# Attention scores as F32 products on 32 rows per head, in place of split products on 128 rows

## The chip, the cores and the metric

The kernel runs on one core of a Trainium2 chip. Its time is the device time of one execution in microseconds (us), less is better. TensorE (PE) multiplies matrices into PSUM, VectorE (DVE), ScalarE (ACT) and GpSimd (POOL) work on tiles, SyncE (SP) issues most DMAs.

## The reference

One transformer block with modulation by a condition, on x of 2 x 2048 x 512, with 16 heads of 32 columns:

```python
mod = jax.nn.silu(condition) @ Wada + bada
sh_a, sc_a, gt_a, sh_m, sc_m, gt_m = jnp.split(mod, 6, axis=1)
xn = _layernorm(x, g1, be1)
xm = xn * (1.0 + sc_a[:, None, :]) + sh_a[:, None, :]
x = x + gt_a[:, None, :] * _attention(xm, Wqkv, Wproj, bproj)
xn = _layernorm(x, g2, be2)
xm = xn * (1.0 + sc_m[:, None, :]) + sh_m[:, None, :]
h = jax.nn.gelu(xm @ W1 + b1, approximate=False)
x = x + gt_m[:, None, :] * (h @ W2 + b2)
```

`_attention` is causal softmax attention: scores of a head are the product of Q (scaled by 32 ** -0.5) and K over 32 columns, masked, exponentiated after the row's maximum is taken off, normalised, and multiplied with V. All inputs are F32.

## The kernel before, in words

The two batches are worked one after the other: a stage that makes Q, K and V (`Qkv.run`, in groups of 512 tokens), an attention stage (`attention_phase`), and a projection (`project_phase`), which for the first batch overlaps the start of the second batch's Q, K, V stage. A feed-forward stage for all tokens comes last. TensorE's products are kept in the order in which the program issues them (`mm`), so the order is written out by hand.

**Q and K.** Each tile of 128 features by 512 tokens is split by `keep` (L854) into a high part and a low part, both F32R: ScalarE copies the high part (L858), VectorE makes the rest (L859), a DMA stores both to `qd` or `kd` in DRAM (L864). `load_keys` and `load_queries` read them back with one head's 32 columns repeated as four row groups, so that the 128 rows of a product hold the four combinations of high and low: the F32R product of `kst` and `qst` on 128 rows is one head's score.

**Attention.** A unit is one of four groups of four heads (`c`) and one block of 512 queries (`i`): 16 units a batch, 32 in all. Each unit has a step per tile of 128 keys, 4i + 3 in all, because the last four tiles are masked and share three steps. In a step (`scores_t`, L574):

- `fold` and `sel`: four BF16 products on 32 rows each, one per head, write minus the row's maximum into the four `st` banks. The maximum stands as three BF16 parts (`split`, L487) in `mhl`, transposed into `fold` by `rows` (L539).
- four `st` products (one per head) add the transposed scores; ScalarE's exponential (L620) turns each into `e`; GpSimd masks the diagonal (L629).
- Between them `row.score` (L517) issues some `s` products: scores not transposed, of units up to three ahead, from which VectorE takes the maximum of each row (L484, masked L479). `count` and `due` set how many fall into a step. They have two PSUM banks of their own, and now and then one of `st`.
- `values` (`o`) multiplies V with `e` of two steps before, and `row_sums` (`sm`) sums `e`: four F32 products each, the four heads in column groups of 32. The order in which these wait is the list `pending`, emptied by `flush` at the end of each step. For unmasked tiles GpSimd first adds the `e` of four key tiles (`begin_chain`, `add_to`, L650), so that one `sm` product serves four.

Scores of the first units are made in the Q, K, V stage already (`among` in `run`): after a projection's product one `s` or two are issued. `sevens` (L964) makes two by two blocks of Q and K by seven products instead of eight and hands its sums to `keep`.

Of the kernel before, what the change touches and what calls it, by code (L numbers as in the profile page):

```python
# [27 lines left out]
def dit_block_kernel(  # L28
# [49 lines left out]
    EE_BUFS = 8  # L78
# [25 lines left out]
    sel = bp.tile([P, P], BF16, tag="sel", name="sel")  # L104
    ident_h = bp.tile([P, P], BF16, tag="ident_h", name="ident_h")
    nc.vector.tensor_copy(ident_h, ident)
# [9 lines left out]
    fold, mhl = [], []  # L116
    for n in range(2):

        f = bp.tile([P, QB + P], BF16, tag=f"fold{n}", name=f"fold{n}")
        fold.append(f)  # L120
    for n in range(AHEAD + 1):
        m = bp.tile([P, HC, HD], BF16, tag=f"mhl{n}", name=f"mhl{n}")
        nc.vector.memset(m, 0.0)
        mhl.append(m)
# [5 lines left out]
    def picks():  # L130
# [32 lines left out]
    qd = [  # L163
        [dram.tile([2, P, T], F32, tag=f"q{b}{c}", name=f"q{b}{c}") for c in range(C)]
        for b in range(B)
    ]
    kd = [
        [dram.tile([2, P, T], F32, tag=f"k{b}{c}", name=f"k{b}{c}") for c in range(C)]
        for b in range(B)
    ]  # L170
# [141 lines left out]
    class Row:  # L312


        def __init__(self, b):
            self.b = b
            self.vv = bp.tile([P, NT, D], F32, tag="vv", name="vv")
            self.kst, self.qst, self.pools = {}, {}, {0: bp}
            self.at = 0
            self.todo = [  # L320
                (u, h, t, kb)
                for u, (_, i) in enumerate(units)
                for h in range(HC)
                for t in range(TQ)
                for kb in range(i + 1)
            ]
            self.mx = None
            self.spent = 0
            self.rows_made = 0

        def load_keys(self, c, g, n=1):

            tok = slice(g * MT, (g + n) * MT)
            if g == 0:
                self.kst[c] = self.pools[c % 2].tile(
                    [P, HC, T], F32R, tag=f"kst{c % 2}", name="kst"
                )
            for r in range(4):
                nc.sync.dma_start(
                    self.kst[c][r * HD : (r + 1) * HD, :, tok].bitcast(F32),  # L340
                    kd[self.b][c][r % 2, :, tok].rearrange("(h d) t -> d h t", d=HD),
                )

        def load_queries(self, u):
            c, i = units[u]
            t = bp.tile([P, HC, QB], F32R, tag="qst", name="qst", bufs=AHEAD + 1)
            for r in range(4):
                nc.sync.dma_start(
                    t[r * HD : (r + 1) * HD].bitcast(F32),
                    qd[self.b][c][r // 2, :, i * QB : (i + 1) * QB].rearrange(  # L350
                        "(h d) t -> d h t", d=HD
                    ),
                )
            self.qst[u] = t
# [48 lines left out]
        def old_queries(self):  # L403

            t = bp.tile([P, HC, QB], F32R, tag="qst", name="qst", bufs=AHEAD + 1)
            return t.bitcast(F32)

        def prefetch(self):

            st = bp.tile([P, HC, T], F32R, tag="kst0", name="kst")
            st = st.bitcast(F32).rearrange("p h t -> p (h t)")
            self.at_s = [
                st[:, n * C * QB : (n + 1) * C * QB].rearrange("p (c q) -> p c q", c=C)
                for n in range(2)
            ]  # L420
            self.xt_s = [st[:, (2 * C + n) * QB : (2 * C + n + 1) * QB] for n in range(TQ)]
            self.wproj = st[:, 3 * C * QB :].rearrange("p (c d) -> p c d", c=C)
            t = self.old_queries()
# [14 lines left out]
        def prepare(self, n):  # L438
# [3 lines left out]
            elif n == 5:  # L442
                ps = rows_of(ps_sp, 0, self.b, "s")
                self.rb_s = [self.old_queries() for _ in range(2)]
# [20 lines left out]
        def bank(self, u, h, t, kb, s):  # L465
            c, i = units[u]
            w, last = self.width(u, h, t, kb)
            mx = self.mx
# [18 lines left out]
        def split(self, u, mx, s):  # L487

            hl = mhl[u % (AHEAD + 1)][:, :, : 4 * TQ].rearrange(
                "p h (t l) -> p h t l", l=4
            )
            mx = mx.rearrange("p (h t) n -> p h t n", h=HC)
            m, rest = [
                s[:, n * HC * TQ : (n + 1) * HC * TQ].rearrange("p (h t) -> p h t", h=HC)
                for n in range(2)
            ]  # L500
            nc.vector.tensor_reduce(m, mx, axis=AX.X, op=ALU.max)
            nc.vector.tensor_reduce(hl[:, :, :, 0], mx, axis=AX.X, op=ALU.max)
            nc.vector.tensor_tensor(rest, m, hl[:, :, :, 0], ALU.subtract)
            nc.vector.tensor_tensor(hl[:, :, :, 1], m, hl[:, :, :, 0], ALU.subtract)
            nc.vector.tensor_tensor(hl[:, :, :, 2], rest, hl[:, :, :, 1], ALU.subtract)  # L505
# [11 lines left out]
        def score(self, n, borrow=None):  # L517

            for k in range(n):
                if borrow and k % 2 == 0:
                    s = borrow()
                else:
                    s = ps_sp.tile([P, QB], F32, tag="s", name="s")
                item = self.todo.pop(0)
                u = item[0]
                if self.mx is None:
                    self.mx = bp.tile(  # L530
                        [P, HC * TQ, units[u][1] + 1], F32, tag="mx", name="mx", bufs=3
                    )
                self.bank(*item, s)
                if not self.todo or self.todo[0][0] != u:
                    self.split(u, self.mx, s)
                    self.mx = None
                    self.at += 1

        def rows(self, u):  # L539
# [3 lines left out]
            ps = ps_sp.tile([P, P], BF16, tag="s", name="ps_m")  # L543
            tc.keep_in_program_order(
                nc.tensor.transpose(
                    ps, mhl[u % (AHEAD + 1)].rearrange("p h r -> p (h r)"), ident_h
                )
            )
# [15 lines left out]
    def attention_phase(row, beside=None):  # L564
        b, vv, kst, qst = row.b, row.vv, row.kst, row.qst
        with pool(f"att{b}") as ap, pool(
            f"ps_st{b}", bufs=HC, space=PSUM
        ) as ps_stp, pool(f"ps_o{b}", space=PSUM) as ps_op:
            row.pools[1] = ap
            among = beside(ap) if beside else None  # L570

            n_bank = [0]

            def scores_t(u, step, n):  # L574

                def st_bank():

                    n_bank[0] += u == len(units) - 1
                    if n_bank[0] % 6 >= HC:
                        return ps_sp.tile([P, QB], F32, tag="s", name="st")
                    return ps_stp.tile([P, QB], F32, tag="st", name="st")
# [3 lines left out]
                q0 = tiles[0][1]  # L593
                w = sum(QB - q for _, q in tiles)
                sts, es = [], []
                for h in range(HC):
                    g = slice(h * HD, (h + 1) * HD)
                    st = st_bank()
                    mm(
                        st[:, :w], sel[g, :], fold[u % 2][g, q0 : q0 + w],  # L600
                        start=True, stop=False,
                    )
                    sts.append(st)
                after = (0, 2) if n > HC else (0, 1)
                if n > HC:
                    row.score(1)
                for h in range(HC):
                    at = 0
# [11 lines left out]
                    act(nc.scalar.activation(e[:, h % 2, :w], sts[h][:, :w], AF.Exp))  # L620
# [14 lines left out]
                    if h in after and n >= 3 or h >= HC - n and n < 3:  # L635
                        row.score(1)
                if n >= 3:
                    row.score(1, st_bank)
                    row.score(min(n, HC) - 3)
                return es, max(0, n - HC - 1)  # L640
# [42 lines left out]
            def flush(upto):  # L683
                while pending and pending[0][0] <= upto:
                    pending.pop(0)[1]()
# [25 lines left out]
            for u, (c, i) in enumerate(units):  # L711
                if NQ <= u + AHEAD < len(units):
                    row.load_queries(u + AHEAD)
                if u % NQ == 0 and c + 1 < C:
                    row.load_keys(c + 1, 0, NG)
                steps = len(steps_of[u])
                for n_step, tiles in enumerate(steps_of[u]):
# [14 lines left out]
                    es, rest = scores_t(u, n_step, n)  # L732
                    rest = len(row.todo) - rest
                    make_rows = False
                    if u + 1 < len(units) and row.rows_made == u + 1:
                        if last:
                            row.score(row.count(cum[-1], u + 1))
# [62 lines left out]
    class Qkv:  # L800
# [46 lines left out]
        def group(self, g, hp, between, among):  # L847
# [35 lines left out]
            if g == 0:  # L883
                n = 0
                for f in range(C):
# [12 lines left out]
                    if f == 0:  # L898
                        asked()
# [1272 lines left out]
```

## Time and profile before

| | |
|---|---|
| median of 3 runs | 2289.31 us (2284.49 to 2290.16) |
| profiled execution | 2284.75 us, span 2283.0 us |
| granted TensorE clock | 0.999 |
| busy: PE, DVE, ACT, POOL | 98%, 68%, 43%, 58% of the span |
| DMA | 355.66 MB, 156 GB/s over the span |

A row of a group names line, engine, operation, written and read tiles, shapes and count, then busy time in us, mean ns of one, and the idle time before it with what ended it. A row of the timeline has start, length, engine, line, operation, tiles, shape and count. `32*128` behind a product's tiles is the part of the array that it uses, rows by columns; x counts records, and an F32 product on TensorE leaves two of them, an F32R or BF16 product one. Lengths of products include their way through the array and overlap, so the time that a product holds the array is read from the start of the next.

### The profile page before, as it was taken

How to read it: one execution, taken by the hardware profiler on the slowest of the kernel's cores; microseconds unless marked ns; L12 is line 12 of the kernel's file. 1: busy time of each engine (PE TensorE's matmuls, PEld its weight loads, DVE VectorE, ACT ScalarE, POOL GpSimd, SP SyncE). 2: the span in 40 equal slices, each digit the busy share in tenths (PEclk: the TensorE clock that was granted, in tenths of full speed). 3: DMA queues.
4: the chain of work that ended last, by engine and by line, in shares of the span. 5: the costliest groups of instructions: out<-in, count | busy, mean ns of one | idle time of the engine just before them, and what ended most of it. 6: DMA issues, size and time to landing. Idle time of an engine off the chain costs nothing. (4 is left out here: it accounts for less than half of the span.)

```text
span 2283.0 us, 34365 instructions
## 1 busy us (share of the span) xinstructions
PE 2237.6 (98%) x12429; PEld 1438.2 (63%) x12429; DVE 1559.3 (68%) x3132; ACT 980.4 (43%) x1908; POOL 1316.9 (58%) x1052
## 2 busy tenths in 40 slices
PE   8999999999999999999999999999999999999998
PEld 3676555455544457654555555447888888888887
DVE  3467776776766525677777777545896876876787
ACT  3334555555555134355555555623422342252230
POOL 4363997888794552268787887463764602602510
PEclk9999999999999999999999999999999999999999
DMA  9769226262234778850512304265466554654643
GB/s 281 240 217 245 54 53 144 54 146 73 76 140 159 243 248 295 267 123 24 121 48 61 84 24 145 97 221 192 146 246 226 196 185 143 210 187 151 205 149 113
DMA packets 134146, 355.66 MB, mean 156 GB/s; under 512 B 14496, under 2 KB 33484, under 8 KB 119256
## 3 DMA queue, kind: packets, MB, share of 16 engines
q1 hardware_dynamic: 126112, 305.18, 44.9%
q0 software_dynamic: 7488, 47.74, 5.7%
q8 instruction: 98, 1.61, 0.3%
q14 instruction: 72, 0.59, 0.1%
q10 hardware_dynamic: 376, 0.55, 0.1%
HBM read 253.80 MB, written 107.48 MB: 158 GB/s over the span
## 5 line engine op out<-in xcount | busy, mean ns | idle before, releaser
L620 ACT ACTIVATE e<-st 128x512 f32<-128x512 f32 (+1 forms) x1152 | 572.9, 579 | 404.7 <-PE st L204 346.0
L484 DVE TENSOR_REDUCE mx<-s 128x1 f32<-128x512 f32 x606 | 409.4, 687 | 192.2 <-PE s L204 190.3
L650 POOL TENSOR_TENSOR ee<-ee,e 128x1024 f32<-128x1024 f32 x212 | 498.7, 2384 | 8.0 <-ACT e L620 8.0
L204 PE MATMUL s<-kst,qst 128*128 128x512 f32 (+3 forms) x1028 | 438.2, 430 | 15.3 <-DVE mx L484 8.7
L204 PE MATMUL st<-qst,kst 128*128 128x512 f32 (+3 forms) x1280 | 400.4, 377 | 0.0
L204 PE MATMUL ps_a<-sum,room 128*128 128x256 f32 x1504 | 356.8, 381 | 4.7 <-DVE c L1655 1.5
L204 PEld LDWEIGHTS ps_a<-sum,room 128*128 128x128 f32 x1504 | 281.2, 190 | 54.4 <-issue 6.0
L204 PE MATMUL o<-e,vv 128*32 128x512 f32 (+3 forms) x2560 | 303.0, 538 | 1.7 <-POOL e L629 1.5
L479 DVE CUSTOM_DVE_ANT_0 junk<-s,causal 128x512 bf16<-128x512 f32 (+3 forms) x422 | 206.9, 490 | 114.5 <-PE s L204 106.5
L204 PEld LDWEIGHTS s<-kst,qst 128*128 128x128 f32 x1028 | 193.0, 188 | 137.4 <-issue 43.6
L204 PEld LDWEIGHTS st<-qst,kst 128*128 128x128 f32 x1280 | 229.1, 188 | 63.2 <-issue 33.9
L650 POOL TENSOR_TENSOR ee<-e 128x1024 f32<-128x1024 f32 x84 | 198.2, 2380 | 112.1 <-ACT e L620 104.2
L629 POOL TENSOR_SCALAR_AFFINE_SELECT e<-e 128x256 f32<-128x256 f32 x256 | 103.9, 435 | 126.2 <-ACT e L620 124.7
L1883 POOL TENSOR_TENSOR c<-c,h 128x512 f32<-128x512 f32 x40 | 58.6, 1484 | 159.4 <-ACT c L1881 159.4
L204 PEld LDWEIGHTS <-sel 32*128 32x128 bf16 x1152 | 29.2, 90 | 190.0 <-issue 187.1
L204 PE MATMUL ps_b<-sum,room 128*128 128x256 f32 x608 | 143.6, 379 | 0.0
L204 PEld LDWEIGHTS o<-e,vv 128*32 128x32 f32 x2560 | 62.4, 108 | 100.9 <-issue 80.5
L204 PEld LDWEIGHTS ps_b<-sum,room 128*128 128x128 f32 x608 | 115.0, 190 | 15.4
L204 PE MATMUL ps_v<-wqkv,xmT 128*128 128x512 f32 x256 | 123.3, 594 | 0.0
L204 PE MATMUL st<-fold,sel 32*128 32x512 bf16 (+1 forms) x1152 | 115.3, 372 | 2.6 <-DVE mhl L505 1.3
L484 DVE TENSOR_REDUCE mx<-st 128x1 f32<-128x512 f32 x162 | 111.1, 686 | 2.8 <-PE st L204 0.4
L1528 POOL TENSOR_TENSOR sum<-xm 128x256 f32<-128x256 f32 x16 | 15.6, 974 | 152.8 <-PE ps_a L204 152.8
(231 smaller groups left out, 3276.2 us busy)
## 6 DMA issues: line engine op xcount, KB each, us to landing
qst<-q SPq DMA_DIRECT2D x128, 256.0 KB
room<-w1e SPq DMA_DIRECT2D x28, 1024.0 KB
kst<-k SPq DMA_DIRECT2D x24, 1024.0 KB
room<-w1e SPq DMA_DIRECT2D x28, 768.0 KB
room<-w2e SPq DMA_DIRECT2D x21, 1024.0 KB
q<-hl SPq DMA_DIRECT2D x32, 512.0 KB
k<-hl SPq DMA_DIRECT2D x32, 512.0 KB
room<-w2e SPq DMA_DIRECT2D x21, 768.0 KB
```

Source lines behind the costliest of these rows:

```text
L204: return tc.keep_in_program_order(nc.tensor.matmul(*args, **kw))
L479: nc.vector.tensor_tensor_reduce(junk[:, :w], s[:, :w], causal[:, QB - w :], 1.0, MASKED, ALU.add, ALU.max, m,)
L484: nc.vector.tensor_reduce(m, s[:, :w], axis=AX.X, op=ALU.max)
L620: act(nc.scalar.activation(e[:, h % 2, :w], sts[h][:, :w], AF.Exp))
L629: nc.gpsimd.affine_select(d, d, pattern=[[0, 2], [1, P]], compare_op=ALU.is_ge, fill=0.0, base=0, channel_multiplier=-1,)
L650: act(engine.tensor_tensor(dst, x, y, ALU.add))
L1528: act(engine.tensor_tensor(dst, x, y, ALU.subtract))
L1883: nc.gpsimd.tensor_tensor(c, c, piece_of(base, i, t, pair), ALU.add)
```

## The change

Q and K stay on chip as they are: `keys_and_queries` allocates four tiles `kT` and four `qT` of 128 features by 2048 tokens in F32 (features of four heads on the partitions), and the Q, K, V stage writes into them (`evict`, and `dst` in `sevens`). `keep`, `load_keys`, `load_queries`, `qd` and `kd` are gone. Every score product is an F32 product of 32 rows by 128 columns in the row group of its head. `fold`, `sel` and the row maximum become F32, with one row per head and query tile in place of three (`join` for `split`).

In a step the heads are staggered: `st` of head h, `fold` with `sel` of head h + 1 (`begin`; after the last head, the first of the next step), then `s` of head h + 2 or h + 3 if one is due (`free`). `o` of two steps before is issued after the second head (`halfway`), `sm` still at the end of the step. GpSimd's sums take two key tiles (`k = n_step % 2`), and there are 16 in place of 8 half buffers of them. `todo` holds the `s` products with the heads innermost, in the order 2, 3, 0, 1.

```diff
-    EE_BUFS = 8
+    EE_BUFS = 16
...
-    sel = bp.tile([P, P], BF16, tag="sel", name="sel")
+    sel = bp.tile([P, P], F32, tag="sel", name="sel")
...
+        def keys_and_queries(self):
+            self.kT, self.qT = [
+                [bp.tile([P, T], F32, tag=f"{n}{c}", name=f"{n}T") for c in range(C)]
+                for n in "kq"
+            ]
...
+            g = slice(h * HD, (h + 1) * HD)
             mm(
                 s[:, :w],
-                self.qst[u][:, h, t * P : (t + 1) * P],
-                self.kst[c][:, h, kb * QB : kb * QB + w],
+                self.qT[c][g, i * QB + t * P : i * QB + (t + 1) * P],
+                self.kT[c][g, kb * QB : kb * QB + w],
                 start=True,
                 stop=True,
             )
...
+            def begin(u, step, h):
+                tiles = steps_of[u][step]
+                q0, w = tiles[0][1], sum(QB - q for _, q in tiles)
+                g = slice(h * HD, (h + 1) * HD)
+                st = ps_stp.tile([P, QB], F32, tag="st", name="st")
+                mm(
+                    st[:, :w], sel[g, :], fold[u % 2][g, q0 : q0 + w],
+                    start=True, stop=False,
+                )
+                folded[u, step, h] = st
...
+                if (u, step, 0) not in folded:
+                    begin(u, step, 0)
                 for h in range(HC):
                     g = slice(h * HD, (h + 1) * HD)
-                    st = st_bank()
-                    mm(
-                        st[:, :w], sel[g, :], fold[u % 2][g, q0 : q0 + w],
-                        start=True, stop=False,
-                    )
-                    sts.append(st)
...
+                    st, at = folded.pop((u, step, h)), 0
                     for j, q in tiles:
                         mm(
-                            sts[h][:, at : at + QB - q],
-                            kst[c][:, h, j * P : (j + 1) * P],
-                            qst[u][:, h, q:],
+                            st[:, at : at + QB - q],
+                            row.kT[c][g, j * P : (j + 1) * P],
+                            row.qT[c][g, i * QB + q : (i + 1) * QB],
                             start=False, stop=at + QB - q == w,
                         )
                         at += QB - q
+                    if h + 1 < HC:
+                        begin(u, step, h + 1)
+                    elif after:
+                        begin(*after, 0)
...
+                    for left in range(n * (h + 1) // HC - n * h // HC, 0, -1):
+                        free = [(h + 2) % HC, (h + 3) % HC]
+                        row.score(n - n * (h + 1) // HC + left, free)
+                    if h == 1:
+                        halfway()
...
-                        k = n_step % TQ
+                        k = n_step % 2
                         if k == 0:
                             even = es
-                        elif k == 1:
+                        else:
                             chain = begin_chain(u, even, es)
-                        else:
-                            add_to(u, chain, es)
-                        if k == TQ - 1 and n_step + 1 < i * TQ:
+                        if k and n_step + 1 < i * TQ:
                             sums_of, wait = (chain, False), 2
...
-            def keep(ps, which, f):
...
+            def evict(ps, which, f):
+                if which:
+                    nc.vector.tensor_copy(row.kT[f][:, tok], ps)
+                else:
+                    nc.scalar.activation(row.qT[f][:, tok], ps, AF.Copy, scale=HD**-0.5)
```

More of the change, by code (lines that the diff above doesn't have):

```diff
@@ L401, in inverses @@
                 self.widen(u - 1)
-        def old_queries(self):
-            t = bp.tile([P, HC, QB], F32R, tag="qst", name="qst", bufs=AHEAD + 1)
-            return t.bitcast(F32)
         def prefetch(self):
[L415 to L423, printed above, removed]
+            self.at_s = [self.old("k0"), self.old("k1")]
+            t = self.old("k2")
+            self.xt_s = [t[:, n, :] for n in range(TQ)]
+            self.wproj = self.old("q0")
+            t = self.old("q1")
             self.next_s = [t[:, n, :] for n in range(TQ)]
@@ L568, in attention_phase @@
         ) as ps_stp, pool(f"ps_o{b}", space=PSUM) as ps_op:
-            row.pools[1] = ap
             among = beside(ap) if beside else None
[L572 to L589, printed above, removed]
+            folded = {}
```

242 lines of the change are left out of this document (92 added, 150 removed).

## The prediction

> **What bounds the kernel now.** I read the page first, then the stages by window, then single steps on the timeline of TensorE. The page:
>
> ```profile
> span 2283.0 us, 34365 instructions
> PE 2237.6 (98%) x12429; PEld 1438.2 (63%) x12429; DVE 1559.3 (68%) x3132; ACT 980.4 (43%) x1908; POOL 1316.9 (58%) x1052
> PEclk9999999999999999999999999999999999999999
> ```
>
> TensorE is busy 98% of the span at a full granted clock; no other engine passes 68%. Five windows cut the span where the kinds of product change (columns: length, PE, PEld, DVE, ACT, POOL busy, clock, DMA share, GB/s):
>
> ```profile
> 60.50:200.80 140.30, 140.15 (x590) 100.20 (x588) 85.72 (x220) 49.89 (x109) 57.06 (x72) 1.00 0.77 238
> 200.80:727.50 526.70, 517.06 (x3627) 260.58 (x3626) 373.02 (x893) 302.93 (x607) 421.58 (x306) 1.00 0.40 102
> 727.50:970.00 242.50, 239.32 (x857) 147.09 (x857) 121.80 (x294) 74.41 (x158) 105.59 (x104) 1.00 0.79 263
> 970.00:1499.00 529.00, 520.99 (x3683) 263.29 (x3683) 373.58 (x893) 304.27 (x610) 405.64 (x282) 1.00 0.32 82
> ```
>
> Attention is the second and the fourth row: 526.7 + 529.0 = 1055.7 us for 288 steps (two batches, four head groups, 3 + 7 + 11 + 15 steps), with TensorE at 98%. The first and third row are the Q, K, V stages, where TensorE is at 99%. What the change is worth is therefore read from the order in which products leave TensorE, not from the other engines. One step of attention:
>
> ```profile
> 562.36 0.47 PE L204 MATMUL s<-kst,qst 128*128 128x512 f32 x1
> 562.75 1.07 PE L204 MATMUL o<-e,vv 128*32 128x512 f32 x8
> 563.75 0.40 PE L204 MATMUL st<-fold,sel 32*128 32x512 bf16 x4
> 564.08 0.50 PE L204 MATMUL st<-qst,kst 128*128 128x512 f32 x1
> 564.41 0.39 PE L204 MATMUL s<-kst,qst 128*128 128x512 f32 x1
> 564.64 0.39 PE L204 MATMUL st<-qst,kst 128*128 128x512 f32 x1
> 564.87 0.28 PE L204 MATMUL s<-kst,qst 128*128 128x256 f32 x1
> ...
> 566.01 1.06 PE L204 MATMUL o<-e,vv 128*32 128x512 f32 x8
> 567.01 0.40 PE L204 MATMUL st<-fold,sel 32*128 32x512 bf16 x4
> ```
>
> The reader should take starts, not durations: 564.41 to 564.64, so a split (F32R) score product of 512 columns on all 128 rows takes the array 0.23 us. Four BF16 row-max products on 32 rows each (563.75 to 564.08) take 0.33 us together: all four stream at once in about the 0.23 us of one product of 512 columns, and 0.10 is the change to whole-array products. The first whole-array product behind them holds for 0.33 instead of 0.23 us, 0.10 for its weights. The step is 3.26 us. Two rounds of four F32 products, heads in column groups, from another place:
>
> ```profile
> 210.90 1.06 PE L204 MATMUL o<-e,vv 128*32 128x512 f32 x8
> 211.78 1.04 PE L204 MATMUL sm<-e,ones 128*32 128x512 f32 x8
> 212.76 0.40 PE L204 MATMUL st<-fold,sel 32*128 32x512 bf16 x4
> ```
>
> Each F32 product has two records, so x8 is four products. The round takes 0.88 us (210.90 to 211.78), and 0.98 where the kind of tiling changes behind it: 0.10 for the change. One F32 product alone is as long as the round of four:
>
> ```profile
> 76.53 1.92 PE L204 MATMUL ps_mod<-wada,sc 128*32 128x512 f32 x16
> 78.39 0.70 PE L204 MATMUL ps_u<-vv,wqkv 128*128 128x256 f32 x2
> 900.71 1.02 PE L204 MATMUL ps_u<-xmT,wqkv 128*128 128x256 f32 x4
> 901.57 1.03 PE L204 MATMUL ps_w<-vv,qst 128*128 128x256 f32 x4
> ```
>
> Four records of 256 columns on the whole array are two F32 products and take 0.86 us (900.71 to 901.57), so 512 columns take 0.86. Hence F32 costs 0.86/0.23 = 3.7 times F32R per column, and four narrow tiles give that back only if all four run at once.
>
> **The change part by part.** *Score products.* A group of 32 rows holds one head. A slot of the changed order is: scores transposed (`st`) of head h, row max (`sel`) of head h+1, then mostly one score product `s` of head h+2 or h+3. The instruction order of the changed kernel has 1152 slots: 844 with one `s` in attention, 136 with two, 171 with none (the last slot of the first batch runs into the next stage). `st` of head h+1 writes on top of the row max of h+1 in the same row group, so it starts when that ends: one F32 product per slot is serial, whatever the others do. I take the slot at the 0.88 us of the round above: 1152 x 0.88 = 1014 us. The 128 slots that are 256 wide would save some 28 us of it, and 86 slots whose `s` falls into the row group of their own `st` or `sel` give about that back.
>
> *The other rounds.* `o` stays. In rounds of 512 columns it is 272 rounds, `sm` is 104; at 0.88 us that is 239 and 92 us. Sums of two key tiles in place of four bring 48 more `sm` rounds (384 products against 192): +42, so 134 us.
>
> ```profile
> L204 PE MATMUL sm<-ee,ones 128*32 128x512 f32 x384 | 52.3, 604 | 0.0
> L650 POOL TENSOR_TENSOR ee<-ee,e 128x1024 f32<-128x1024 f32 x212 | 498.7, 2384 | 8.0 <-ACT e L620 8.0
> L484 DVE TENSOR_REDUCE mx<-s 128x1 f32<-128x512 f32 x606 | 409.4, 687 | 192.2 <-PE s L204 190.3
> L620 ACT ACTIVATE e<-st 128x512 f32<-128x512 f32 x1024 | 531.3, 603 | 366.8 <-PE st L204 316.3 <-PE s L204 27.6 <-POOL ee L650 8.9
> ```
>
> GpSimd is rid of 84 of its adds, 84 x 2.38 = 200 us, which nothing waits for while TensorE sets the pace.
>
> *Changes of tiling.* Row tiles and column tiles alternate; whole-array products all but vanish from attention. `o` now stands in the middle of a step and `sm` at its end, so the order has 404 column phases against 284. Each costs 0.10 + 0.02 to enter and 0.10 + 0.10 (change, first weights) to leave: 404 x 0.32 = 129 us. The 30 transposes of the row max on the whole array cost two changes each, some 0.5: 15 us.
>
> *Waits.* By the same prices attention before is: row max 272 rounds x 0.23 = 63, `st` 1088 (in products of 512 columns) x 0.23 = 250, `s` 960 x 0.23 = 221, changes 288 x 0.46 = 132 (0.20 behind the row max, 0.16 from 562.36 to 562.75 beyond the 0.23, 0.10 behind `o`), `o` 239, `sm` 92, transposes 5: 1002 us. Measured are 1055.7, so 54 us of waits hide between records. A slot (0.88) is longer than a reduce (0.69) or an exponential (0.60), yet `s` has two banks, and a bank is free only 0.88 + 0.69 after its product starts; everything on TensorE stands in line behind an `s` that waits for one. Two banks give one `s` per (0.88 + 0.69) / 2 = 0.79 us, under the slot, so I keep the 54 us as they are; bounds are 0 and twice that. `o` in the middle of a step reads exponentials from two steps before: over 5 us old, and nothing waits there.
>
> Attention after: 1014 + 239 + 134 + 129 + 15 + 54 = 1585 us, +529.
>
> *Score products in the Q, K, V stages.*
>
> ```profile
> 900.29 0.58 PE L204 MATMUL s<-kst,qst 128*128 128x512 f32 x1
> 902.25 0.41 PE L204 MATMUL s<-kst,qst 128*128 128x128 f32 x1
> 902.50 1.08 PE L204 MATMUL ps_w<-vv,fold 128*128 128x256 f32 x4
> 0.00:200.80 200.80, 48.47 (x81) 15.33 (x81) 47.08 (x88) 1.00 0.81 249
> 727.50:970.00 242.50, 48.13 (x81) 15.32 (x81) 47.60 (x89) 1.00 0.79 263
> ```
>
> Now a lone F32R `s` among whole-array F32 products holds the array 0.42 us at 512 columns (900.29 to 900.71) and 0.25 at 128: 0.37 at their mean of 404. The last two rows count them (PE column, tile `s` alone): 81 in each stage. The changed order has 82 in each, in 74 runs, 66 of them lone: a lone one is a row tile in a whole-array stream, so 0.68 of streaming, and a change with first weights on both sides, 4 x 0.10: 1.08. 148 x (1.08 - 0.37) - 16 x 0.37 = +99 us.
>
> *At nothing.*
>
> ```profile
> L859 DVE SCALAR_TENSOR_TENSOR hl<-ps_w,hl 128x512 fp32r<-128x512 f32 x24 | 16.3, 681 | 1.8 <-ACT hl L858 1.8
> L858 ACT ACTIVATE hl<-ps_w 128x512 fp32r<-128x512 f32 x24 | 14.3, 594 | 65.1 <-DVE ps_w L995 59.7 <-DMA q<-hl 5.1
> ```
>
> The high and low halves (64 tiles, one ScalarE pass of 0.59 and one VectorE pass of 0.68 us each), their stores to and loads from DRAM, the three-way split of the row max: all ran beside TensorE at 98 to 99%. Without them SyncE's queue no longer stands in front of the stores of `sums` and `o`, whose readers come thirteen units later. Were TensorE not the pace, 64 x 0.68 = 44 us would be their worth, a fall and not a rise. Late next is nothing that I see: VectorE loses work.
>
> Sum: the profiled execution took 2284.75 us (span 2283.0, 1.75 around it); + 529 + 99 = 2913. The median of the runs is 2289.31, 0.2% over the profiled one; I forecast **2910 us**.
>
> [...] What the trace shows of two F32 products in different groups is the first modulation, where the third of four products has to wait for its weights' DMA (records of that tile alone, PE in the second column):
>
> ```profile
> 11.10:11.16 0.06, 0.02 (x2) 0.03 (x2) 0.00 (x0) 1.00 1.06 410
> 11.89:11.92 0.03, 0.03 (x3) 0.02 (x1) 0.00 (x0) 1.00 0.72 273
> 11.98:12.01 0.03, 0.03 (x5) 0.03 (x2) 0.00 (x0) 1.00 1.10 341
> ```
>
> Two first halves run at 11.14; a third product's first half starts at 11.90; the second halves of the first two start only at 11.99. So the array lets a later product pass the waiting second half of an earlier one. [...]
>
> **The rivals.** *Better overlap.* If queued products of other row groups run ahead and the banks allow it, a step costs each row group its own three products, 3 x 0.88 = 2.64 us, in place of four slots, 3.52: 288 x 0.88 = 253 less, **2660 us**. For it: the pass shown at 11.90. Against it: two `s` banks, and column phases that make all groups meet every half step. 0.16.
>
> *Start in order.* A product per 0.44 us (half of 0.88): row max, `st` and `s` of attention are 1088 + 1088 + 960 = 3136 products of 512 columns, 3136 x 0.44 = 1380 in place of 1014: **3276 us**. Against it: the rows at 11.90. 0.08.
>
> *No overlap of row groups in F32.* 3136 x 0.88 = 2760: **4656 us**. Against it: the BF16 row, four in 0.33. 0.04.
>
> *Faster.* No row shows F32 on 32 rows. Should a product there stream in one pass, as BF16 does, a slot is 0.22 and attention 1585 - 1152 x 0.66 = 825 (VectorE's 373 in each window would still fit), and the stages between lose 24 in place of 99: 2284.75 - 231 + 24 = **2078 us**. It decides from a slot of 0.38: the loss of 529 + 99 = 628 is then won back by 1152 slots and some 114 slots' worth of lone `s`, (1152 + 114) x 0.50. Against it: F32 on 32 columns takes two records of 0.43 as on 128. 0.05. Packing alone cannot bring it: at best four in 0.88 equal F32R's 0.23 each, and the row max goes from 0.23 to 0.88 per step.
>
> **How the numbers follow.** Forecast 0.66, within which the waits (-54 or +54) and first weights that no slot hides (1152 x 0.10 = +115, or none) give 2856 to 3079. The range takes in the better overlap and its error and leaves out 3276, 4656 and 2078: **2620 to 3100 us**. This kernel's measurement can tell some 0.3% from no change. Faster 0.05, same 0.01, slower 0.94 (0.66 + 0.16 + 0.08 + 0.04).
>
> **What would show it.** Right: the two windows of attention at about 790 us each, TensorE at 98%, starts of `st` 0.88 us apart within a half step, every `st`, `sel` and `s` with two records on 32*128, the Q, K, V stages 50 us longer each, the stages behind attention unchanged. Wrong: `st` starts 0.65 apart or less (better overlap), one record per product (faster), 0.44 between neighbouring products' starts (in order), or TensorE idle in attention, with VectorE or the banks of `s` named as releaser.

## The result, and the profile after

The changed kernel took **2962.7 us** (median of 4 runs, 2961.4 to 2963.7) against 2287.7 us (4 runs, 2284.5 to 2290.2): a ratio of 1.295, with a 95% interval of 1.293 to 1.297. The forecast was 2910 us, in a range of 2620 to 3100.

The page of the kernel after:

```profile
span 2960.2 us, 41653 instructions
PE 2932.4 (99%) x16525; PEld 1565.5 (53%) x16525; DVE 1552.6 (52%) x2935; ACT 1035.1 (35%) x1876; POOL 1120.6 (38%) x968
PEclk9999999999999999999999999999999999999999
```

TensorE was at 98% and is at 99%, at a full clock, in a span that is 677 us longer. GpSimd lost 196 us of work and no other engine passes 53%, and none of that shortened the span. The same five windows as before, moved to where the kinds of product change now (length, PE, PEld, DVE, ACT, POOL busy, clock, DMA share, GB/s):

```profile
60.50:265.00 204.50, 204.50 (x678) 103.97 (x676) 72.51 (x185) 42.65 (x98) 58.94 (x73) 1.00 0.23 69
265.00:1071.00 806.00, 804.90 (x5643) 323.56 (x5645) 386.42 (x833) 339.66 (x606) 328.91 (x271) 1.00 0.11 36
1071.00:1367.00 296.00, 296.00 (x889) 146.59 (x881) 103.93 (x254) 63.94 (x141) 99.96 (x97) 1.00 0.35 126
1367.00:2176.00 809.00, 807.90 (x5655) 324.96 (x5655) 386.44 (x833) 342.48 (x611) 309.12 (x241) 1.00 0.07 23
2176.00:2960.20 784.20, 769.41 (x3525) 642.48 (x3523) 586.50 (x783) 228.74 (x388) 296.40 (x241) 1.00 0.55 184
```

Attention takes 806 + 809 = 1615 us (1055.7 before): +559. The Q, K, V stages take 204.5 and 296.0 us (140.3 and 242.5): +118. What follows attention takes 784.2 us, and took 784.0 (2283.0 - 1499.0). 559 + 118 is the whole difference of the spans, 677 us.

One half step and the column phase behind it, on the timeline of TensorE (start, length; each F32 product has two records):

```profile
622.17 0.69 PE L194 MATMUL st<-qT,kT 32*128 32x512 f32 x1
622.18 0.69 PE L194 MATMUL st<-fold,sel 32*128 32x512 f32 x1
622.19 0.71 PE L194 MATMUL s<-kT,qT 32*128 32x512 f32 x2
622.71 0.59 PE L194 MATMUL st<-qT,kT 32*128 32x512 f32 x1
622.71 0.59 PE L194 MATMUL st<-fold,sel 32*128 32x512 f32 x1
622.72 0.61 PE L194 MATMUL s<-kT,qT 32*128 32x512 f32 x2
623.14 0.59 PE L194 MATMUL st<-qT,kT 32*128 32x512 f32 x1
623.15 0.59 PE L194 MATMUL st<-fold,sel 32*128 32x512 f32 x1
623.57 0.59 PE L194 MATMUL st<-qT,kT 32*128 32x512 f32 x1
623.58 0.59 PE L194 MATMUL st<-fold,sel 32*128 32x512 f32 x1
624.10 1.07 PE L194 MATMUL sm<-ee,ones 128*32 128x512 f32 x8
625.09 0.69 PE L194 MATMUL st<-qT,kT 32*128 32x512 f32 x1
```

Read the starts. The program's order here is `st` of head 2, row max of head 3, `s` of head 0 (the first slot), then `st` of head 3, row max of head 0, `s` of head 1 (the second slot), then `sm`. At 622.17 four products start together, each in a row group of its own: `st` of head 2, the row max of head 3, and both `s`. Their second records start at 622.71 and end the slot at 623.14: 0.97 us, two records of 0.43 and some 0.1 that I put down to the first weights. The `st` of head 3, which adds to the row max in its own row group, starts only then (623.14); its slot takes 0.96 us to the column phase at 624.10, two records of 0.43 and 0.1 that I put down to the change. The `s` of head 1 stands behind that `st` in the order of instructions, and ran 0.95 us ahead of it, so in the second slot two of the four row groups are empty. Half step and column phase take 2.92 us (622.17 to 625.09).

### The profile page after: what moved, and what is told of

The parts are those of the page before. It is cut to its first block, busy times and chain, and to the rows that moved or that the text cites. A ratio compares the mean times of both kernels' runs of the same rounds, so it can differ in the third digit from the quotient of the medians.

```text
span 2960.2 us, 41653 instructions
## 1 busy us (share of the span) xinstructions
PE 2932.4 (99%) x16525; PEld 1565.5 (53%) x16525; DVE 1552.6 (52%) x2935; ACT 1035.1 (35%) x1876; POOL 1120.6 (38%) x968
## 4 chain that ended last, share of the span: by engine, by line
PE 95%; DVE 4%; issue 1%; DMA 0%; POOL 0%; ACT 0%; SPq 0%; DVEq 0%; POOLq 0%; ACTq 0%
PE st L194 25%; PE s L194 18%; PE ps_a L194 11%; PE o L194 9%; PE ps_b L194 6%; PE sm L194 5%; PE ps_v L194 4%; PE ps_o L194 3%; PE ps_u L194 3%; PE ps_c L194 3%; PE ps_w L194 2%; PE ps_qk L194 2%; DVE sum L1462 1%; PE ps_xt L202 1%; DVE h L1589 1%
## 5 line engine op out<-in xcount | busy, mean ns | idle before, releaser
L194 PE MATMUL s<-kT,qT 32*128 32x512 f32 (+3 forms) x2560 | 1050.4, 565 | 1.8 <-DVE mx L443 1.2
L194 PE MATMUL st<-qT,kT 32*128 32x512 f32 (+3 forms) x2560 | 987.8, 546 | 0.0
L194 PE MATMUL st<-fold,sel 32*128 32x512 f32 (+1 forms) x2304 | 849.2, 605 | 0.0
L448 DVE TENSOR_REDUCE mx<-s 128x1 f32<-128x512 f32 x768 | 528.6, 691 | 551.4 <-PE s L194 304.0
L590 POOL TENSOR_TENSOR ee<-e 128x1024 f32<-128x1024 f32 x168 | 395.2, 2353 | 603.6 <-ACT e L560 602.6
L194 PEld LDWEIGHTS st<-qT,kT 32*128 32x128 f32 x2560 | 399.2, 184 | 406.6 <-issue 372.9
L194 PEld LDWEIGHTS s<-kT,qT 32*128 32x128 f32 x2560 | 366.4, 183 | 289.8 <-DVE mx L448 116.7
L443 DVE CUSTOM_DVE_ANT_0 junk<-s,causal 128x128 bf16<-128x128 f32 (+3 forms) x512 | 251.3, 491 | 380.3 <-PE s L194 198.5
L194 PEld LDWEIGHTS st<-fold,sel 32*128 32x128 f32 x2304 | 271.7, 183 | 30.9 <-issue 14.9
L590 POOL TENSOR_TENSOR ee<-ee,e 128x1024 f32<-128x1024 f32 x44 | 102.5, 2351 | 0.0
```

The source lines that it names most:

```text
L194: return tc.keep_in_program_order(nc.tensor.matmul(*args, **kw))
L443: nc.vector.tensor_tensor_reduce(junk[:, :w], s[:, :w], causal[:, QB - w :], 1.0, MASKED, ALU.add, ALU.max, m,)
L448: nc.vector.tensor_reduce(m, s[:, :w], axis=AX.X, op=ALU.max)
L590: act(engine.tensor_tensor(dst, x, y, ALU.add))
```

## The experiments

Each kernel changes what its diff shows, and nothing else unless the text says so. The kernel before ran on the same chip in each set; its medians there were 2286.8 to 2287.3 us. The changed kernel was not run again there, so differences from its 2962.7 us rest on these medians agreeing with the 2287.7 us of its own set.

### A third bank for `s`

```diff
-            f"ps_st{b}", bufs=HC, space=PSUM
+            f"ps_st{b}", bufs=HC - 1, space=PSUM
...
+            if self.extra and self.n_bank % 3 == 0:
+                s = self.extra.tile([P, QB], F32, tag="s3", name="s")
```

> The changed kernel with a third PSUM bank for s, taken from the four of st. Chain theory: no change, 2945 to 2980 us (or slower, if three st banks are too few). Bank theory: an s of the next slot no longer stands in front of the queue without a bank; the slots shorten where two s fall together, 2880 to 2920 us.

Measured: **2891.4 us** (2 runs, 2890.2 to 2892.5), 71 less. The groups of weight loads for `s` (busy, mean ns, then the idle time before them and what ended it), first of the changed kernel, then with the third bank:

```profile
L194 PEld LDWEIGHTS s<-kT,qT 32*128 32x128 f32 x2560 | 366.4, 183 | 289.8 <-DVE mx L448 116.7 <-issue 88.7 <-DVE mx L443 67.2
```

```profile
L194 PEld LDWEIGHTS s<-kT,qT 32*128 32x128 f32 x2560 | 358.6, 183 | 171.1 <-issue 95.5 <-DVE mx L449 39.6 <-DVE mx L444 18.5
```

Idle time that a reduce on VectorE ended fell from 184 to 58 us. Waits for the two banks of `s` were worth at least 71 us, although the changed kernel's TensorE shows 99% busy: its records leave 27.8 us of the span open in all (2960.2 - 2932.4), so most of these 71 us left no gap there.

### Sums over four key tiles again

```diff
-                        k = n_step % 2
+                        k = n_step % TQ
...
+                        else:
+                            add_to(u, chain, es)
```

There are 8 half buffers of the sums again, as in the kernel before.

> The changed kernel with GpSimd's sums over four key tiles as before. 48 rounds of sm and 48 column phases fewer: 48 x (0.88 + 0.20 to 0.32) = 52 to 58 us less, 2905 to 2911 us, if GpSimd (then some 200 us more busy in attention) still hides behind TensorE. If GpSimd becomes late: 2930 us or more.

Measured: **2907.4 us** (2 runs, 2906.5 to 2908.2), 55 less, as expected. So the 48 more rounds of `sm` in the changed kernel cost 55 / 48 = 1.15 us each: the round's 0.88 and most of the 0.32 of a column phase.

### Fewer and longer runs of `s` in the Q, K, V stages

```diff
-                        row.scores(row.count(cum[0] * past, 0))
+                        due = row.count(cum[0] * past, 0)
+                        row.scores(due if due >= 2 else 0)
```

The same is done at the stage's other place that calls `scores`; 78 runs are left of 148.

> The changed kernel with the scores of the Q, K, V stages issued only when two are due. 78 runs of s in place of 148 in the stream of whole-array products. Each run less saves its changes and one F32 product that now runs beside another: 70 x 1.08 = 76 us, 2890 us, if the price of a lone s is what the forecast took. If a second s in a run waits for its bank or costs a product of its own: 2930 us or more.

Measured: **2907.3 us** (2 runs, 2907.1 to 2907.6), 55 less where 73 were expected: 55 / 70 = 0.79 us for a run that goes. Part of what is missing shows in the trace: the edit also makes eight runs of three `s`, which take 1.29 to 2.96 us each up to the next whole-array product. At the price of a run of two of the same widths (0.42 to 1.06) they would take 11 us less together. That the third product waits for one of the two banks would explain it; no run tests that. The lone `s` itself is as forecast. On the timeline of the changed kernel, in the second stage:

```profile
1246.01 0.69 PE L194 MATMUL s<-kT,qT 32*128 32x256 f32 x2
1246.63 1.99 PE L194 MATMUL ps_u<-vv,old 128*128 128x256 f32 x8
1248.55 0.69 PE L194 MATMUL s<-kT,qT 32*128 32x256 f32 x2
```

From one `s` to the next are 2.54 us, of which four products of 256 columns take 4 x 0.43 = 1.72: 0.82 us for an `s` of 256 columns, 0.43 for its two records and 0.39 more, which the forecast has as two changes and their first weights (0.40, an estimate).

### The row max in three BF16 parts

```diff
-    sel = bp.tile([P, P], F32, tag="sel", name="sel")
+    sel = bp.tile([P, P], BF16, tag="sel", name="sel")
...
+            nc.vector.tensor_tensor(rest, m, rows[:, :, :, 0], ALU.subtract)
+            nc.vector.tensor_tensor(rows[:, :, :, 1], m, rows[:, :, :, 0], ALU.subtract)
+            nc.vector.tensor_tensor(rows[:, :, :, 2], rest, rows[:, :, :, 1], ALU.subtract)
```

`fold`, the row-max rows and their transposes are BF16 with it, as in the kernel before.

> The changed kernel with the row maximum back in three BF16 parts (sel, fold and split as before); score products stay F32 on 32 rows. Chain theory (a slot is as long as one F32 product because st stands behind the F32 row max of its head in the same row group): behind a BF16 row max of 0.23 us the two slots of a half step can run side by side, 0.23 + 0.88 in place of 2 x 0.88, so 576 half steps x 0.65 = 374 us less: 2590 us. Bank theory (the two banks of s, each held for the product and its reduce, hold up everything behind an s): two s of a half step share the two banks and the next pair must wait 0.88 + 2 x 0.69 + about 0.25, about 2.5 us per half step where it now takes 2.8 with its share of column phases; so at most some 0.3 us of a half step can be won: 2963 - 576 x 0.15 to 0.3 = 2790 to 2875 us.

Measured: **2984.6 us** (2 runs, 2973.8 to 2995.3): no gain, so both theories missed. The page's clock line shows what neither had, and three neighbouring windows show its form (the clock is the third number from the right):

```profile
PEclk9999997989889999999888989899999999999999
```

```profile
675.10:678.51 3.41, 3.05 (x13) 0.75 (x15) 2.69 (x10) 2.01 (x4) 0.86 (x1) 1.00 0.00 0
678.51:681.93 3.42, 3.42 (x17) 1.24 (x10) 0.52 (x1) 0.00 (x0) 1.49 (x1) 0.50 0.02 5
681.93:685.34 3.41, 2.79 (x25) 1.29 (x21) 1.20 (x5) 1.08 (x2) 2.04 (x1) 1.00 0.00 0
```

TensorE's clock is granted at half for whole stretches of 3.41 us, 294 us of this span in all, so some 147 us of work at full speed were lost, an estimate that takes TensorE for the pace throughout. Taken off, the span of 2993.6 is 2847 us, inside the 2790 to 2875 of the theory of banks. That is arithmetic behind a miss; later runs had to show it.

What brings the clock down? I added up for each stretch of 3.41 us, on the grid on which the clock changes, how much of the array its products fill: rows x columns / 128 x 128, times 0.43 us for a record of 512 columns in F32, 0.23 in F32R, 0.22 in BF16 (603.65 to 603.87 in the run after this one). In the stretch from 675.10 that is 0.31, although TensorE was busy for 3.05 of its 3.41 us. Over the traces of all thirteen kernels (before, after and these eleven), from 30 us on, there are some 10,280 such stretches. 352 are followed by one at half clock; a border of fill at 0.375 tells these from the others with 29 exceptions, all of them between 0.34 and 0.39. Half clock itself lowers the fill of a stretch: on this run's timeline the next `st` starts 0.40 us behind a BF16 row max at half clock (679.91 to 680.31) and 0.22 at full clock (673.73 to 673.95). So take alone the 9,922 stretches that were at full clock: 103 are followed by half clock, and the same border has 12 exceptions. The busy share doesn't tell them apart: its best border leaves 81 of these 103 wrong, and the stretches that brought a full clock down in this run were 50 to 100% busy. The changed kernel comes down to 0.42 and stays clear.

### The BF16 row max with the third bank

Both edits above.

> The changed kernel with the row max in three BF16 parts as in the run before, and the third bank for s as well. Theory: the BF16 row max saved 119 us of work, but the clock was granted at half for 299 us of that run (150 us lost); it falls for 3.41 us behind each stretch of 3.41 us in which products fill less than about 0.36 of the array, and the waits for two banks make these stretches. With three banks the waits go, the clock stays above 0.99, and the gains add: 2891 - 119 = 2772, down to 2710 where the shorter steps were more bound by banks. Rival, BF16 products between F32 ones take the clock down by themselves, whatever waits: clock near 0.95 again and 2870 to 2920 us. Rival, no clock but no gain either (BF16 in row groups is not shorter): 2880 to 2900 at a clock of 1.00.

Measured: **2765.7 us** (4 runs, 2744.3 to 2769.0). The profiled run, the shortest, has a clock of 0.991 and half clock for 41 us in place of 294; the other three have 0.983 to 0.984, so some 90 us at half clock each. The theory's 2772 holds for the time, its clock above 0.99 for that one run alone: the two gains add, once most of the half clock is gone, and with it most of the idle time of the weight loads of `s` that a reduce ended (286 us without the third bank, 109 with it). A half step of this run on the timeline:

```profile
603.64 0.69 PE L196 MATMUL st<-qT,kT 32*128 32x512 f32 x1
603.65 0.38 PE L196 MATMUL st<-fold,sel 32*128 32x512 bf16 x1
603.65 0.69 PE L196 MATMUL s<-kT,qT 32*128 32x512 f32 x1
603.66 0.39 PE L196 MATMUL st<-fold,sel 32*128 32x512 bf16 x1
603.87 0.89 PE L196 MATMUL st<-qT,kT 32*128 32x512 f32 x2
...
605.04 1.07 PE L196 MATMUL sm<-ee,ones 128*32 128x512 f32 x8
```

The second `st` starts 0.23 us behind the first and 0.22 behind the row max in its own row group (603.65), and the half step takes 1.40 us (603.64 to 605.04), though some of its `s` are 128 columns wide, in place of 1.92 in the run with three banks (600.80 to 602.72 on its timeline). Not every half step gains as much: the mean gain is 125 us (2891 to 2766), where all 576 would give 576 x 0.52 = 300.

### The F32 row max alone, in the kernel before

```diff
-    sel = bp.tile([P, P], BF16, tag="sel", name="sel")
+    sel = bp.tile([P, P], F32, tag="sel", name="sel")
...
-                hl = hp.tile([P, 2, MT], F32R, tag="hl", name="hl", bufs=4)
+                hl = hp.tile([P, 2, MT], F32R, tag="hl", name="hl", bufs=3)
```

The tiles for `o` and the sums on their way out have one buffer for two.

> The kernel before with one part of the change alone: the row max as one F32 row per product instead of three BF16 parts (scores stay F32R on 128 rows; to make room, the high and low halves have three buffers for four, the two output tiles one for two). Theory: four F32 products in four row groups run side by side in the two passes of one, 0.86 us, in place of 0.22; in before nothing can run beside them, since the scores behind them take the whole array. 272 rounds x 0.65 = +177, and 30 F32 transposes about +6: 2470 us (2450 to 2490), a quarter of the loss of 675. Rival, products of different row groups start in order, one per 0.44 us: 272 x 1.43 = +389, 2677 us. Rival, the row max is hidden or not at fault: within 10 us of 2288.

Measured: **2514.4 us** (4 runs, 2510.7 to 2516.2), +228, 24 over the range's end. Windows of its attention, and one round on the timeline:

```profile
216.00:840.00 624.00, 616.72 (x4202) 293.39 (x4204) 366.66 (x835) 301.05 (x606) 423.51 (x307) 0.99 0.34 86
1102.00:1724.00 622.00, 614.66 (x4206) 293.04 (x4206) 367.06 (x838) 302.17 (x608) 400.36 (x277) 1.00 0.27 68
```

```profile
626.36 1.14 PE L202 MATMUL st<-fold,sel 32*128 32x512 f32 x8
627.43 0.51 PE L202 MATMUL s<-kst,qst 128*128 128x512 f32 x1
```

Attention takes 1246 us, +190, where 183 were expected. Four F32 row-max products take 1.07 us to the next product (0.33 in BF16), where 0.98 was taken. The other 35 us are in the Q, K, V stages (from 60.5 to 216.0 and from 840 to 1102), 15 and 20 longer. In the second TensorE waits 16.8 us for tokens that ScalarE normalises (`ps_xt` on `x`, five waits; the kernel before has none there), and its clock is at half for 17 us. In the first that wait is 2 us, but less was done ahead of it: 121 records of TensorE by 60.5 us, where the kernel before has 151. This kernel has a buffer less for the halves there, so I put the 35 us down to my edit, not to the row max; no run takes the two apart. Products in order, at 2677, are excluded.

### One pass per score product

```diff
-                [bp.tile([P, T], F32, tag=f"{n}{c}", name=f"{n}T") for c in range(C)]
+                [bp.tile([P, T], F32R, tag=f"{n}{c}", name=f"{n}T") for c in range(C)]
```

This is the run with the BF16 row max, and Q and K in F32R.

> The run with the BF16 row max, and Q and K kept as F32R on the same 32 rows: one pass a product in place of two records of 0.43. It leaves out the low halves of Q and K, so the scores have F32R's precision. Layout, order of instructions, sums and stages are those of the changed kernel. Theory: the loss is the passes. A slot falls from 0.97 us (first weights, two serial F32 products) to about 0.22 + 0.23; 1152 slots x 0.5 = some 580 less than 2963, with the lone s of the Q, K, V stages 50 less, and banks for s then the next limit (0.46 us each with two): 2200 to 2400 us, at the kernel before. Rival, the row groups, changes of tiling and the stagger cost by themselves: above 2550 us. The clock may fall as the array is filled less; that adds up to 5%.

Measured: **2529.3 us** (4 runs, 2522.3 to 2536.2), 129 over the range and under the rival's 2550: missed as it stands. The clock was 0.902, half clock for 495 us, all of it in attention (the next run's expectation puts it at 481). Half of that is 248: some 2281 us without it, in the middle of the range, by the same estimate as above. I had allowed the clock 5%; it took 10. Against the run with the BF16 row max (2984.6), from which only the type of Q and K differs, one pass a product is worth 455 us, with 200 us more at half clock.

### One pass, three banks, pairs

The one-pass run with the third bank and the longer runs of `s` in the stages.

> The one-pass run (Q and K as F32R on 32 rows without their low halves, row max in three BF16 parts) with the third bank for s, and scores of the Q, K, V stages only where two are due. Theory: the one-pass run would have taken 2288 us at a full clock (2529 less half of its 481 us at half clock), and the clock falls where products fill less than 3/8 of the array over 3.41 us, which the waits for banks bring about. With the third bank these waits go: half clock for under 100 us, attention shorter by some 25 us a window, the stages by some 25 us together: 2215 to 2290 us, for the first time no slower than the kernel before. Rival, one-pass products on 32 rows fill the array too little whatever waits: clock near 0.90 again, 2430 to 2480 us.

Measured: **2267.4 us** (6 runs, 2262.9 to 2283.2), ratio 0.992 to the kernel before, 95% interval 0.990 to 0.995: 0.8% shorter, which counts as the same time, and the only kernel here that is not slower, though its scores leave out the low halves of Q and K. Its attention:

```profile
215.80:720.00 504.20, 467.17 (x3819) 174.07 (x3820) 375.48 (x889) 306.17 (x605) 323.16 (x266) 0.95 0.17 54
968.50:1474.00 505.50, 468.34 (x3828) 174.69 (x3831) 376.02 (x889) 307.27 (x607) 302.00 (x235) 0.94 0.10 32
```

Half clock fell to 109 us from 495, a little over the 100 expected at most. 504 and 506 us a window against 806 and 809: with the packing, the stagger, the layout and the sums of the changed kernel, one pass a product brings attention under the 527 and 529 of the kernel before.

### The three single improvements together, in F32

> The changed kernel (F32 everywhere) with the three single improvements together: third bank for s (-71), sums over four key tiles (-55), scores of the Q, K, V stages only where two are due (-55). Theory, they are separate costs: 2963 - 181 = 2782 us (2765 to 2800). Rival, they overlap (with fewer column phases the banks matter more, or what waits hid comes out): 2820 us or more. The clock: fewer waits and fewer products fill the array alike, 0.99 or more expected.

Measured: **2781.7 us** (4 runs, 2777.7 to 2787.6), clock 0.997 to 1.00: the expected 2782. They are separate costs.

### And the BF16 row max on top

> The changed kernel with all that can be mended without touching its scores: three banks for s, sums over four key tiles, Q, K, V stages' scores in pairs (2782 us together) and the row max in three BF16 parts. Theory: the BF16 row max is worth the 119 to 150 us it was worth before, at a clock above 0.99: 2630 to 2680 us; what is left of the loss, some 350 us, is that of F32 scores on 32 rows. Rival, with sums over four key tiles fewer full rounds fill the array, and the clock falls: below 0.98, 2700 us or more.

Measured: **2687.3 us** (4 runs, 2683.7 to 2700.0), clock 0.978 to 0.983: neither range. The row max brings 94, not 119 or more; 85 us at half clock cost some 43, so the work fell by some 137. The lower clock that the rival expected is there, but it cost less than the rival said.

### Another order of the step

```diff
+                    if h % 2 == 0:
+                        begin(u, step, h)
+                        begin(u, step, h + 1)
```

With three banks for `s`: row max of heads 0 and 1, their `st`, then `s` of others; then heads 2 and 3 the same; `o` and `sm` in one column phase per step.

> The run with a third bank for s (2891 us, F32 throughout), with the step in another order: row max of heads 0 and 1, their st, s of the others, row max of heads 2 and 3, their st, s of the others, and o and sm in one column phase per step instead of one behind each half. Theory: a half step costs 1.92 us because s of both halves passes the waiting st in its first 0.97 us and leaves two row groups empty in the second; in the new order the row max of heads 2 and 3 runs beside the st of heads 0 and 1, and about 120 column phases go (x 0.32 = 37 us): 2740 to 2790 us, towards the 2660 of the prediction's rival of better overlap. Rival, one serial product per head sets the slot whatever the order: 2850 to 2890 us (the phases alone). The clock above 0.99 by both.

Measured: **3099.4 us** (4 runs, 3081.4 to 3107.2), 208 more than the run with three banks, where both theories expected less. TensorE's waits, and a place on its timeline:

```profile
PE st L194 <- ACT e L566: 134.3, 200, 0.8
```

```profile
628.11 0.59 PE L194 MATMUL st<-fold,sel 32*128 32x512 f32 x1
629.42 0.69 PE L194 MATMUL st<-fold,sel 32*128 32x512 f32 x1 [0.72 <-ACT e L566]
629.42 0.69 PE L194 MATMUL st<-qT,kT 32*128 32x512 f32 x1
```

The order opens two row maxes at once, and the third bank of `s` was taken from `st`: the fourth row max waits for an exponential, 134 us, by far the longest wait of TensorE, and its clock was at half for 133 us, where both theories had it above 0.99. The wait and half of the 133 come to some 200 of the 208 us, an estimate. The order and the lack of a bank aren't told apart by this run; whether the order would help with four banks for `st` stays open.

## Why the prediction was right

**What bounds it.** Right: TensorE stayed the pace, at 99%, and the work of the other engines that went (196 us on GpSimd alone) brought nothing. Nor did larger errors cancel: the two terms below that were off were both too small.

**The slot.** Right. Half step and column phase were forecast at 2 x 0.88 + 0.88 + 0.32 = 2.96 us and are 2.92 where nothing waits. The reason given, one F32 product per slot that is serial, is in the rows: `st` at 622.17 and 623.14. That reason had to be tested, since a step limited by products in order or by the banks could have shown a similar length: with a short row max the next `st` starts 0.23 us later (603.64, 603.87).

**Waits.** The term that was mis-sized. I kept the 54 us of the kernel before, because two banks give an `s` each 0.79 us and a slot takes 0.88. But two `s` start at once (622.19) and the next slot has none: the supply is right on the average and not when it is asked. The third bank took 71 us away; the bound of 108 holds. With it attention is 1585 - 54 + 71 = 1602 of the 1615 measured; the other 13 stay open.

**Sums.** +42 was the rounds alone; undone they gave 55, because their column phases, which stand in another term, go too. The sum has both.

**Q, K, V stages.** +99 forecast, +118 measured. The price of a lone `s` after the change was right (0.82 for 256 columns, 0.83 by the forecast's terms). What a lone F32R `s` cost before was read too high, 0.42 us at 512 columns. In the kernel before:

```profile
192.38 1.02 PE L204 MATMUL ps_v<-wqkv,xmT 128*128 128x512 f32 x2
192.84 0.80 PE L204 MATMUL s<-kst,qst 128*128 128x512 f32 x1
193.47 1.02 PE L204 MATMUL ps_v<-wqkv,xmT 128*128 128x512 f32 x2
```

From one `ps_v` to the next are 1.09 us, of which its two records take 0.86, so the `s` between them cost 0.23 and no more. Its start at 192.84 lies 0.46 us behind that of the `ps_v` ahead of it, whose two records take 0.86, so the time from its start to the next start (0.63) is not what it holds. The forecast's own lines say the same: from 901.57 to 902.50 are 0.93 us, 0.86 for two F32 products of 256 columns and 0.07 for the `s` of 128, where 0.25 was taken. At 0.18 for the mean of 404 columns in place of 0.37 the forecast's sum gives +130, 12 over the +118 measured. A tally of starts in both stages gives some 0.22 us a product before and 1.07 a run after.

**At nothing.** Right: the stages behind attention differ by 0.2 us, and no new wait for a store or a load shows.

**The rivals.** Start in order (3276) is excluded by the row at 622.19, where an `s` starts 0.95 us ahead of an `st` (623.14) that stands before it in the order; the trace before shows the like for column groups (11.90 ahead of 11.99). Better overlap (2660) did not come: what runs ahead is `s`, and then it is missing. No overlap (4656) is excluded by four starts within 0.02 us. The faster rival named the right quantity, the passes: with one pass, a BF16 row max, three banks and pairs the same order of the step takes 2267 us, though not the 2078 of its sum. Some 55 us of that are the clock's; the rest stays open.

**The whole loss.** From 2963 to 2288: 181 us are banks, sums and lone `s` (2782 without them), 94 the F32 row max (2687, with what the clock then took), and 399 the rest, which one pass a score product wins back and 20 us more (2267, from the run at 2687 by the type of Q and K and sums over two key tiles, which by themselves cost 55). So the two records of F32 on 32 rows are over half of the loss; packing four of them into the array does not repay them.

## What to carry to other kernels

Price a packed product by its passes first: four F32 products of 32 rows side by side took two records of 0.43 here, 0.86 us, hardly less than four F32R products on the whole array at 0.23 each, and an `st` that waited for the row max in its own row group made the slot serial (622.17 to 623.14). Ask not only how many buffers a stage needs on the average but how many it asks for at once, and don't take 99% busy as proof that nothing waits: at 99% a third bank still took 71 us away, and two of four row groups were empty in a slot. Read what a product costs from the time between two products of its surroundings, with and without it, and not from its own start. When work is taken off TensorE and the time does not fall, look at the granted clock before looking for another theory: in the run with the BF16 row max it was at half for 294 us.

## What the runs showed of the hardware that was not expected

- In these traces the granted clock went with how full the array was, not with how long TensorE was busy: a border at 0.375 of fill tells the stretches of 3.41 us that were followed by one at half clock from the others (some 10,280 stretches, 29 exceptions), and the one from 675.10 of the run with the BF16 row max, filled to 0.31 and followed by half clock, was busy for 3.05 us. Half clock took some 147 us of that run and 248 of the one-pass run, both estimates. The border was first put at 0.36, from that first run; in the seven runs made after it, 264 of 5,377 stretches are followed by half clock, and 0.36 has 39 exceptions. How full a changed kernel would be was harder to forecast: the third bank took half clock from 294 to 41 us, and from 495 to 109 with pairs, near what was expected, but the clock of the one-pass run, the run in another order and the run with all but the scores was missed. No run changed the fill alone.
- In this case products in different row groups passed one another in F32 too: an `s` started 0.95 us ahead of an `st` that stands before it in the order (622.19, 623.14).
